# Moving work between the regimes of a graph-attention kernel: weight sums, aggregation steps and a softmax placed elsewhere

## The chip, the cores and the metric

The kernel runs on one core of one Trainium2 chip. The core has engines that work side by side, each through its own list of instructions in order: TensorE (PE in the profile, with its weight loads as PEld) multiplies matrices into the PSUM banks, VectorE (DVE) and ScalarE (ACT) work on elements, GpSimd (POOL) too, and SyncE (SP) issues the transfers. An engine waits where the next instruction of its list needs what another has not yet delivered. The metric is the device time of one launch in microseconds, the median of several runs. Before the change it is 1914.68 us (three runs from 1913.48 to 1915.18).

## What is computed

There are 64 graphs of 256 nodes with 512 features. Two layers follow each other, each with a residual and a layer norm over the features:

```python
# layer 0: neighbours averaged by degree, both halves multiplied by W
deg = jnp.sum(adj, axis=-1, keepdims=True)
agg = jnp.einsum('bij,bjf->bif', adj, x) / jnp.maximum(deg, EPS)
out = jnp.einsum('bnf,of->bno', jnp.concatenate([x, agg], axis=2), W)
x = _layernorm(x + jax.nn.relu(out), axis=-1)

# layer 1: a score for each node, a softmax over the 256 nodes of a graph
q, k = jnp.split(x @ Wqk, 2, axis=-1)
v = x @ Wv
agg = jnp.einsum('bij,bjd->bid', adj, k * mask[:, :, None])
w = inv_scale * mask * jnp.einsum('bid,bid->bi', q, agg)
x = _layernorm(x + jax.nn.softmax(w, axis=1)[:, :, None] * v, axis=-1)
```

## The kernel before

The graphs are taken in 32 pairs, and each turn of the loop, called a period here, does layer 0 of pair j and layer 1 of pair j - 1 in alternation. In layer 1 the product of the two halves of Wqk is formed once, so that a score is a row of x times that product times the aggregated x.

Every product is done by Strassen's method in Winograd's form: seven half-size products in place of eight, from sums of blocks of both factors. The sums of the weights W0 (layer 0) and W1 (layer 1) are made once at the start; those of x, of the adjacency and of the intermediate results in every period. The first two products and the fifth of an outer Strassen step are themselves split once more ("inner").

VectorE, ScalarE and GpSimd instructions keep the order in which the program writes them. Work that may lie anywhere, such as norms, degrees or sums, is put into named chains; a clock of the program, advanced by every product and used at build time only, decides after which product the next step of a chain is written:

```python
class InOrder:
    # ... (free: the modelled time at which this engine is done)
            self.free = max(self.free, self.clock[0]) + self.cost(name, size)
            return self.tc.keep_in_program_order(getattr(self.engine, name)(out, *args, **kwargs))
# ...
    def tick():                      # after a product: write steps that fit
        while not quiet[0]:
            for c in list(chains):   # chains in order of rank
                if c[2][0] <= clock[0] and c[3][0][0].free <= clock[0] + room[c[3][0][0]]:
                    step(c)
                    break
            else:
                return

    def flush(*names):               # write the rest of these chains now
        # ...
```

The sums of a weight are sixteen subtractions, four of them 1024 elements wide and twelve 256 wide:

```python
    def weight_sums(w, name):
        # ... b11, b21, b12, b22: quarters of w; t1, t2, t4, it: new tiles
        def inner_of(n, p, b):
            # ... c11 ... c22: quarters of b
            return [sub(i1, c12, c11), sub(i2, c22, i1), sub(c12, c22, c12), sub(i4, c21, i2)]
        work = ([sub(t1, b12, b11)] + inner_of(0, "P1", b11) + [sub(t2, b22, t1)] + inner_of(2, "P5", t1)
                + [sub(b12, b22, b12), sub(t4, b21, t2)] + inner_of(1, "P2", b21))
```

The profile leaves numbers out of names, so the tiles of both weights read as w, t and t_i.

Aggregation with the adjacency is called gather. Its seven steps have the letters a to g; tv are sums of the right factor, sa those of the adjacency:

```python
        def g5():                                    # c
            twice(p5, "S1", "T1")
        def u2():                                    # d
            twice(u, "S2", "T2", start=False)
            act.copy(r12, of(u))
        def u3():                                    # e
            twice(u, "S3", "T3", start=False)
            act.copy(r22, of(u))
            vec.tensor_add(r22, of(p5), r22)
        def g3():                                    # f
            twice(p5, "S4", "B22", start=False)
            vec.tensor_add(r12, of(p5), r12)
```

The step f adds on to the bank p5 that step e's addition has read before. The degrees of a pair need the adjacency by rows, which lies in the tile turn; ScalarE sums each row:

```python
        def degree(k, t):
            act.activation(r[:, k, t], r[:, k, t], AF.Copy, accum_out=deg[:, k, t:t + 1])
        def invert():
            vec.tensor_scalar(rdeg, deg, DEG_EPS, None, op0=OP.max)
            vec.reciprocal(rdeg, rdeg)
```

The norm of layer 0 is a chain of VectorE and ScalarE steps for each half of the graph: scale by the degree, residual (both scalar_tensor_tensor), statistics (bn_stats, bn_aggr), factor (ScalarE), shift (VectorE), scale (ScalarE), and the turning of the result (transpose into the tile turn, then 16 small transfers into x1T, which layer 1 multiplies).

The softmax of a pair takes the maximum, two exponentials for each graph, a reciprocal and a product, and then queues the additions of v to x ("adds") and the last norm ("finish"):

```python
        queue(0, "softmax", (vec, lambda: vec.reduce_max(top, rk, axis=AX.XY, negate=True)),
              (act, lambda: exp(0)), (act, lambda: exp(1)), (vec, divide))    # divide ends with finish(j)
```

For the last pair the softmax is done in another way: the scores are turned by TensorE (transpose), and the probabilities come out of a small product with the reciprocal of the total:

```python
        def divide(to):
            vec.reciprocal(total, total)
            for t in range(NT):
                tc.keep_in_program_order(nc.tensor.matmul(to[:, t:t + 1], e[:, t * P:(t + 1) * P], total, ...))
```

In the loop, run("i k ...") writes the products named by letters in that order; m, p, q, r, s belong to layer 0, and j, k, h, n, q, p and f to layer 1:

Of the kernel before, what the change touches and what calls it, by code (L numbers as in the profile page):

```python
# [94 lines left out]
def resnorm_kernel(  # L95
# [34 lines left out]
    clock, chains, shared, quiet = [0.0], [], [1.0], [False]  # L130
# [28 lines left out]
    def flush(*names):  # L159
        while True:  # L160
            c = next((c for c in chains if not names or c[1] in names), None)
            if not c:
                return
            step(c)

    def run(order, **units):
        for name in order.split():
            units[name].pop(0)()
# [87 lines left out]
    def weight_sums(w, name):  # L256


        b11, b21, b12, b22 = (w[:, k * H:(k + 1) * H, :] for k in range(4))
        t1, t2, t4 = (const.tile([P, H, F], F32, name=f"{name}{k}") for k in (1, 2, 4))  # L260
        it = const.tile([P, 3, 3, HF], F32, name=f"{name}i")
        sides = {"B22": b22, "T2": t2, "T3": b12, "T4": t4}
        sub = lambda *args: lambda: vec.tensor_sub(*args)

        def inner_of(n, p, b):
            c11, c12, c21, c22 = (b[:, e, h * HF:(h + 1) * HF] for e in range(2) for h in range(2))
            i1, i2, i4 = (it[:, r, n] for r in range(3))
            sides[p] = {"B11": c11, "B21": c21, "B22": c22, "T3": c12, "T1": i1, "T2": i2, "T4": i4}
# [3 lines that stand above are left out]
        return sides, work  # L272
# [35 lines left out]
    def mask_adj(j):  # L308
        def mask(k, t):
            act.activation(adjs[j][:, k, t], adjs[j][:, k, t], AF.Copy,  # L310
                           scale=mask_sb[:, 2 * j + k, t:t + 1])
        queue(4, "mask", *[(act, lambda k=k, t=t: mask(k, t)) for k in range(2) for t in range(NT)])

    def degrees(j):
        deg = small.tile([P, 2, NT], F32, name="deg")
        rdeg = rdegs[j] = small.tile([P, 2, NT], F32, name="rdeg")
        r = rows.pop(j)
# [7 lines that stand above are left out]
        queue(2, "degrees", *[(act, lambda k=k, t=t: degree(k, t)) for k in range(2) for t in range(NT)],  # L325
              (vec, invert))
# [335 lines left out]
    inner_sums(Xs[0], gp, 1)  # L662
    sumsA[0] = adj_sums(0)
    degrees(0)
    W1, work = weight_sums(w1, "t1_")
    queue(9, "w1", *[(vec, do) for do in work])
    pu, py, pf, pw = banks
# [2 lines left out]
    for j in range(NP):  # L670
        X = Xs.pop(j)
        flush("finish")
        owns[j] = pool.tile([P, 2, NT, F], F32, name="own", bufs=3)
        if j > 0:
            load_adj(j)
            run_now(late_sums)
            late_sums.clear()
            sumsA[j] = adj_sums(j)

        u, y, o = pf, py, pu  # L680
        ys[j] = pool.tile([P, 2, NT, F], F32, name="y")
        a1, a2, a3, a4, a5, a6, a7 = layer0(j, o, u, y)
        i = inner("P1", X, W0, pw[0], u, a1)
        k = inner("P5", X, W0, pw[1], y, a5)
        m = inner("P2", X, W0, pw[0], o, a2)
        p, q = pairs(u, X, S2, W0["T2"], a6), pairs(u, X, S3, W0["T3"], a7)
        r, s = pairs(y, X, S4, W0["B22"], a3), pairs(u, X, A22, W0["T4"], a4)
        if j == 0:
            run("i k i k i k i k", i=i, k=k)
            flush("degrees")  # L690
            load_rows(1)
        elif j == 1:
            run("i k i k i k i k", i=i, k=k)
            run("m p p m p p m", m=m, p=p)
            flush("norm")
            places[0](range(16))
        else:
            run("i f k", i=i, k=k, f=open1)
            send_scores(j - 2)
            run("i f k", i=i, k=k, f=open1)  # L700
            flush("norm")
            fetch_scores(j - 2)
            places[0](range(16))
            run("i f k i f k", i=i, k=k, f=open1)
        if j > 0:
            flush("mask")
            sumsM[j - 1] = adj_sums(j - 1)
            load_x(j)
            if j + 1 < NP:
                load_rows(j + 1)  # L710
        if j > 1:
            softmax(j - 2)
            shared[0] = 1.0
        if j != 1:
            run("m p p m p p m", m=m, p=p)
        run("q q q q m", m=m, q=q)
        if j > 0:
            Y = x1Ts.pop(j - 1)
            inner_sums(Y, gp, 0)
            sums_Y = (*outer_sums(Y, vec), (vec, lambda: inner_sums(Y, gp, 1)))  # L720
        if j > 1:
            queue(1, "sums", *sums_Y)
        run("r r r r", r=r)
        T = sums_T(ys[j])

        if j != 1 and j < NP - 1:
            degrees(j + 1)
        zs[j] = pool.tile([P, 2, NT, F], F32, name="z")
        g = gather(sumsA.pop(j), T, zs[j], pw[1], y[1], y[0])

        def load_next():
            if j == NP - 1:
                return
            if j > 0:
                load_xT(j + 1)
                shared[0] = 1.25
            inner_sums(Xs[j + 1], gp, 0)
            rest = outer_sums(Xs[j + 1], gp)
            run_now(rest[:1])
            inner_sums(Xs[j + 1], gp, 1)  # L740
            late_sums.extend(rest[1:])
        if j == 0:
            load_next()
            run("s s a b s c d e s g f", s=s, **g)
        else:
            u2, o2, y2 = o, pf, y
            b1, b2, b3, b4, b5, b6, b7, b8 = layer1(j - 1, ys[j][:, :, 0], o2, u2, y2)
            jj = inner("P1", Y, W1, pw[0], u2)
            k = inner("P2", Y, W1, y[0], o2, b2)
            if j == 1:  # L750
                run("s s a b s c d e s g f", s=s, **g)
                flush("w1")
                degrees(2)
                queue(1, "sums", *sums_Y)
                run("j k j k j k j", j=jj, k=k)
                b1(None)
                run("k", k=k)
            else:
                run("s s j a b s j c d s j e k j", s=s, j=jj, k=k, **g)
                quiet[0] = True  # L760
                run("k", k=k)
                quiet[0] = False
                b1(None)
                run("g f", **g)
        flush("softmax", "adds", "sums", "degrees")
        if j > 0:
            aggs[j - 1] = late.tile([P, 2 * N_SIDE], F32, name="agg").rearrange(
                "p (k t f) -> p k t f", k=2, t=NT)
            vs[j - 1] = [late.tile([P, NT, F], F32, name="v", bufs=2) for _ in range(2)]
            T = sums_T(owns[j - 1])  # L770
            g = gather(sumsM.pop(j - 1), T, aggs[j - 1], pw[0], o2[1], o2[0])
            h, q = pairs(u2, Y, S2, W1["T2"], b6), pairs(u2, Y, S3, W1["T3"], b7)
            n = inner("P5", Y, W1, pw[1], y2, b5)
            p, open1 = pairs(u2, Y, A22, W1["T4"], b4), pairs(y2, Y, S4, W1["B22"], b3)
            norm0(j)
            mask_adj(j)
            run("k h h" if j > 1 else "h h", k=k, h=h)
            load_next()
            run("n k" if j > 1 else "n", k=k, n=n)
            run("h h a n b q d q n c q e q p n g p f p", h=h, n=n, q=q, p=p, **g)  # L780
            b8()
            run("p", p=p)
            py, pu = pu, py
        else:
            norm0(0)
            mask_adj(0)


    j = NP - 1
# [27 lines left out]
    run("c d i m e i m g i f i", i=i, m=m, **g)  # L817
    v = pool.tile([P, 2, NT, F], F32, name="z")
    vs[j] = [v[:, k] for k in range(2)]
    run("m n h h", m=m, n=n, h=h)  # L820
    softmax(j - 1)
    run("m n h h n q q q q n", h=h, m=m, q=q, n=n)
    flush("softmax", "adds")
    run("p p p p", p=p)
    w = small.tile([P, 2, NT], F32, name="w", bufs=1)
# [4 lines left out]
        turn()  # L830
        exps()
    run("r r", r=r)
    flush()
    probs[j] = small.tile([P, 2, NT], F32, name="probs", bufs=2)
    for k in range(2):
        last[k][0](pw[k])
        vec.tensor_copy(probs[j][:, k], pw[k][:, :NT])
        b3(k)
    norms = []

    def close(k, t, scale):
# [40 lines left out]
```

## Time and profile before

| what | number |
|---|---|
| device time, median | 1914.68 us |
| span of the profiled execution | 1913.8 us |
| PE busy | 1881.3 us (98%) |
| PEld busy | 1248.8 us (65%) |
| DVE busy | 1587.1 us (83%) |
| ACT busy | 1061.6 us (55%) |
| POOL busy | 748.8 us (39%) |
| mean granted TensorE clock | 0.994 |
| moved by the transfers | 182.17 MB, 95 GB/s |

A share of busy time is an average over the whole span. The table says that TensorE is the busiest engine, but not where it waits. For that one takes three views: the waits, which give for each engine, tile and line what it waited for, how long in total and how often; the table by stretch, with the busy time of every engine in parts of the span; and the timeline, which lists the instructions of one engine in order, with the idle time before each and what ended it. Nearly all instructions have the same two lines, 90 (the recording helper) and 173 (the products), so they are told apart by their tiles: y and own are results of layer 0, z and agg those of the two gathers, v the values of layer 1, tv and sa the gather's sums.

### The profile page before, as it was taken

To read this page: it belongs to the slowest core of one execution; us is meant where nothing else is said; L and a number is where in the kernel's file an instruction comes from. 1 tells how busy PE (TensorE), PEld (TensorE's weight loads), DVE (VectorE), ACT (ScalarE), POOL (GpSimd) and SP (SyncE) were. 2 spreads that over 40 slices of the span, in tenths; PEclk is the share of its full clock that TensorE was granted. 3 is DMA by queue.
4 is the path that set the end of the run, shared out by engine and by line. 5 is a ranking of instruction groups with operands and counts; after the bars stand their busy time and mean duration, and the time that the engine had idled before them with its cause. 6 is when DMAs were issued, how large, how long until landed. Compare 5 with 4: busy or idle time off the path is not lost.

```text
span 1913.8 us, 22655 instructions
## 1 busy us (share of the span) xinstructions
PE 1881.3 (98%) x6596; PEld 1248.8 (65%) x6596; DVE 1587.1 (83%) x2952; ACT 1061.6 (55%) x2571; POOL 748.8 (39%) x898
## 2 busy tenths in 40 slices
PE   9899999999999999999999999999999999999996
PEld 4566666666666666666676666666666666666663
DVE  6879878889888888888889888888888898888885
ACT  3455555565555565655565655555655655555654
POOL 4344324444334444234444244443244343244420
PEclk9999999999999999999999999999999999999998
DMA  6223343433433423434433434433434333434311
GB/s 221 63 56 97 105 102 76 116 82 94 105 96 89 116 76 97 105 84 104 113 76 99 105 75 114 101 84 103 105 72 116 87 95 107 98 80 116 80 52 46
DMA packets 389147, 182.17 MB, mean 95 GB/s; under 512 B 272160, under 2 KB 353696, under 8 KB 389024
## 3 DMA queue, kind: packets, MB, share of 16 engines
q1 hardware_dynamic: 389024, 180.72, 36.4%
q8 instruction: 54, 0.88, 0.2%
q14 instruction: 69, 0.57, 0.1%
HBM read 114.10 MB, written 34.06 MB: 77 GB/s over the span
## 4 chain that ended last, share of the span: by engine, by line
PE 86%; DVE 5%; DMA 3%; POOL 2%; SPq 2%; issue 1%; ACT 1%; ACTq 0%; DVEq 0%; POOLq 0%
PE bank L173 86%; SPq L178 2%; DMA turn<-adj 1%; DVE own L90 1%; DMA xT<-x_t 1%; POOL xT_i L90 1%; POOL sa L90 1%; POOL xT_s L90 1%; DVE st L90 1%; DVE y L90 0%; ACT own L90 0%; DVE bank L90 0%; DMA x1T<-turn 0%; DVE tv L90 0%; DVE t_i L90 0%
## 5 line engine op out<-in xcount | busy, mean ns | idle before, releaser
L90 ACT COPY bank<-bank 128x256 f32<-128x256 f32 (+1 forms) x576 | 251.9, 437 | 248.5 <-PE bank L173 232.5
L90 POOL TENSOR_TENSOR xT_i<-xT 128x256 f32<-128x256 f32 x62 | 61.4, 990 | 530.7 <-DMA xT<-x_t 443.4
L173 PE MATMUL bank<-w,x1T_s 128*128 128x512 f32 x512 | 260.3, 592 | 0.0
L173 PE MATMUL bank<-w,xT_s 128*128 128x512 f32 x512 | 230.2, 592 | 1.3 <-DVE y L90 1.3
L90 ACT ACTIVATE own<-own,shift,rstd 128x512 f32<-128x512 f32 x256 | 197.8, 808 | 12.3 <-DVE shift L90 12.1
L90 POOL TENSOR_TENSOR x1T_i<-x1T 128x256 f32<-128x256 f32 x64 | 49.7, 776 | 393.2 <-DMA x1T<-turn 379.3
L173 PE MATMUL bank<-tv,sa 128*128 128x256 f32 x768 | 191.9, 379 | 1.4 <-issue 1.4
L90 DVE TENSOR_TENSOR y<-bank,y 128x512 f32<-128x512 f32 x192 | 128.6, 684 | 61.5 <-ACT y L90 57.2
L173 PEld LDWEIGHTS bank<-tv,sa 128*128 128x128 f32 x768 | 145.8, 190 | 49.2 <-issue 18.7
L90 ACT COPY y<-bank 128x512 f32<-128x512 f32 x192 | 109.1, 587 | 119.4 <-PE bank L173 116.7
L90 DVE BATCH_NORM_STATS2 st<-own 128x6 f32<-128x512 f32 x256 | 173.1, 676 | 2.4
L173 PEld LDWEIGHTS bank<-w,xT_s 128*128 128x128 f32 x512 | 97.2, 190 | 96.7 <-issue 86.0
L173 PE MATMUL bank<-t,xT_s 128*128 128x512 f32 (+1 forms) x384 | 158.8, 522 | 0.5 <-ACT own L90 0.5
L173 PE MATMUL bank<-t,x1T_s 128*128 128x512 f32 (+1 forms) x384 | 158.1, 521 | 0.3 <-ACT y L90 0.3
L90 ACT ACTIVATE turn<-turn 128x256 f32<-128x256 f32 x128 | 52.5, 411 | 174.0 <-DMA turn<-adj 174.0
L90 DVE TENSOR_TENSOR bank<-bank,fifth 128x256 f32<-128x256 f32 x256 | 97.3, 426 | 49.4 <-PE bank L173 45.2
L90 ACT COPY agg<-bank 128x512 f32<-128x512 f32 x128 | 74.6, 583 | 96.7 <-PE bank L173 95.9
L173 PE MATMUL bank<-t,x1T 128*128 128x512 f32 x256 | 125.2, 592 | 0.0
L90 POOL TENSOR_TENSOR sa<-adj 128x256 f32<-128x256 f32 x128 | 108.7, 849 | 36.0 <-ACT adj L90 27.4
L173 PE MATMUL bank<-t,xT 128*128 128x512 f32 x248 | 121.6, 592 | 0.0
L173 PE MATMUL bank<-t_i,x1T_i 128*128 128x256 f32 x384 | 114.8, 381 | 2.5 <-ACT bank L90 2.3
L173 PE MATMUL bank<-t_i,xT_i 128*128 128x256 f32 x384 | 115.4, 382 | 0.2
(144 smaller groups left out, 4172.3 us busy)
## 6 DMA issues: line engine op xcount, KB each, us to landing
x<-x SPq DMA_DIRECT2D x64, 512.0 KB, 4.9
xT<-x_t SPq DMA_DIRECT2D x62, 512.0 KB, 6.2
x1T<-turn SPq DMA_DIRECT2D x496, 64.0 KB, 2.3
out<-own SPq DMA_DIRECT2D x62, 512.0 KB, 4.8
adj<-adj_t SPq DMA_DIRECT2D x64, 256.0 KB, 3.0
turn<-adj SPq DMA_DIRECT2D x64, 256.0 KB, 5.1
row<-d SPq DMA_DIRECT2D x31, 256.0 KB, 4.7
wqk<-wqk_t SPq DMA_DIRECT2D x4, 512.0 KB, 5.5
```

Of the source, the lines that this page charges most:

```text
L90: return self.tc.keep_in_program_order(getattr(self.engine, name)(out, *args, **kwargs))
L173: tc.keep_in_program_order(nc.tensor.matmul(ps, a, b, start=start, stop=True, skip_group_check=True))
L178: return tc.keep_in_program_order(nc.sync.dma_start(out, in_))
```

## The change

The change moves instructions; none is added or taken away. It has four parts.

- **Sums of W1.** Before their chain is queued, the modelled time of VectorE (vec.free) is set to six microseconds after the clock. Up to there it had run far ahead, since every sum recorded in the setup counts. So the chain's steps are written sooner, beside the first products of period 0. What is left of the chain is held back during the end of that period and put back after it.
- **Aggregation steps.** In periods 0 and 1 the order of the steps changes from "a b s c d e s" to "a b c d s e s": a product s now stands between d and e.
- **Degrees of pair 2.** They are queued in period 1 after the norm, and not ahead of the first products of layer 1.
- **Softmax of the pair next to last.** It is queued four products sooner, and the remaining chains are written out after the last pair's probabilities and no longer ahead of them.

```diff
+    vec.free = clock[0] + 6.0
     W1, work = weight_sums(w1, "t1_")
     queue(9, "w1", *[(vec, do) for do in work])
@@ period 0
             load_next()
-            run("s s a b s c d e s g f", s=s, **g)
+            held = [c for c in chains if c[1] == "w1"]
+            chains[:] = [c for c in chains if c[1] != "w1"]
+            run("s s a b c d s e s g f", s=s, **g)
@@ period 1
-                run("s s a b s c d e s g f", s=s, **g)
+                run("s s a b c d s e s g f", s=s, **g)
                 flush("w1")
-                degrees(2)
                 queue(1, "sums", *sums_Y)
@@ periods from 1 on, layer 1
             run("k h h" if j > 1 else "h h", k=k, h=h)
+            if j == 1:
+                degrees(2)
+                flush("degrees")
             load_next()
@@ end of period 0
             norm0(0)
             mask_adj(0)
+            chains.extend(held)
@@ last pair
-    run("m n h h", m=m, n=n, h=h)
     softmax(j - 1)
-    run("m n h h n q q q q n", h=h, m=m, q=q, n=n)
+    run("m n h h m n h h n q q q q n", h=h, m=m, q=q, n=n)
     flush("softmax", "adds")
@@
     run("r r", r=r)
-    flush()
     probs[j] = small.tile([P, 2, NT], F32, name="probs", bufs=2)
     for k in range(2):
         last[k][0](pw[k])
         vec.tensor_copy(probs[j][:, k], pw[k][:, :NT])
         b3(k)
+    flush()
```

## The prediction

> **What bounds the kernel now.** I started with the list of waits, taken for TensorE alone. Its columns are the waiting engine, tile and line, what it waited for, the total in us, how often, and the longest.
>
> ```profile
> PE bank L576 <- DVE total L90: 4.9, 2, 3.9
> PE bank L173 <- DVE z L90: 4.0, 1, 4.0
> PE bank L173 <- ACT bank L90: 2.9, 6, 1.7
> PE bank L173 <- DVE y L90: 1.6, 2, 1.3
> PE bank L566 <- DVE w L90: 1.5, 1, 1.5
> PE bank L173 <- issue: 1.4, 2, 0.7
> ```
>
> All of TensorE's waits together are under 20 us of 1913.8. The table by stretch says where they lie (after the stretch and its length: busy us of PE, PEld, DVE, ACT, POOL, then granted clock, DMA share, GB/s).
>
> ```profile
> 30.00:40.00 10.00, 10.00 (x29) 5.32 (x28) 4.15 (x10) 5.03 (x15) 0.84 (x2) 1.00 0.37 107
> 50.00:57.00 7.00, 2.96 (x11) 1.78 (x11) 6.93 (x10) 1.76 (x3) 5.62 (x6) 0.85 0.00 0
> 57.00:64.00 7.00, 6.89 (x20) 5.08 (x20) 6.79 (x10) 2.63 (x8) 0.00 (x0) 0.66 0.00 0
> 130.00:600.00 470.00, 469.76 (x1657) 313.64 (x1656) 393.69 (x735) 267.77 (x654) 187.01 (x224) 1.00 0.38 97
> 1890.00:1900.00 10.00, 4.10 (x14) 1.86 (x12) 6.66 (x22) 4.93 (x12) 0.00 (x0) 0.90 0.14 51
> ```
>
> The reader is to see three regimes. From 130 to about 1890 us TensorE never stops: nothing that this change does elsewhere can shorten that part, and nothing there can swallow a gain made ahead of it, because work that arrives earlier is simply multiplied earlier. Before 130 us and after 1890 us VectorE sets the pace. And at 30 to 40 us VectorE is idle for almost six of ten microseconds, just before the stretch where TensorE waits for it.
>
> The timeline shows the wait itself, first TensorE, then VectorE (start, length, engine, line, operation; in brackets the idle time before it and what ended it):
>
> ```profile
> 51.57 1.11 PE L173 MATMUL bank<-tv,adj 128*128 128x256 f32 x4
> 56.73 2.05 PE L173 MATMUL bank<-y,sa 128*128 128x256 f32 x4 [4.04 <-DVE z L90]
> 58.57 1.06 PE L173 MATMUL bank<-t_i,xT_i 128*128 128x256 f32 x2
> ```
>
> ```profile
> 37.07 0.69 DVE L90 TENSOR_TENSOR y<-bank,y 128x512 f32<-128x512 f32 x1 [5.00 <-ACT y L90]
> 48.97 2.31 DVE L90 TENSOR_TENSOR t<-w,t 128x1024 f32<-128x1024 f32 x1
> 57.63 1.21 DVE L90 TENSOR_TENSOR t<-w,t 128x1024 f32<-128x1024 f32 x1
> 1898.18 0.16 DVE L90 SCALAR_TENSOR_TENSOR shift<-mv,rstd 128x2 f32<-128x2 f32 x1 [2.01 <-ACT rstd L90]
> ```
>
> The last aggregation product of period 0 (bank<-y,sa, step f) needs the second addition into z. VectorE gives that at 56.58, because it has put sums of W1 between: t at 48.97 and four quarter sums at 52.59. The last line is the tail: the softmax of the last pair stands behind a shift of the pair before it.
>
> **What the Trainium skill says.** "TensorE: Matmul & The Clock Gate", Part 1, What's actually happening, says that the array runs at half clock after about 3.4 us idle and at full clock after as much steady work. The trace agrees: after the 4.04 us gap two matmul pieces start every 0.85 us (58.57, 59.42, 60.27) where they otherwise take 0.43 us, and the granted clock is 0.66 for 57 to 64 us. "SBUF — State Buffer", SBUF: two separate sides, says that VectorE and GpSimd lock each other out of a shared port pair when a VectorE instruction has two SBUF inputs. The trace agrees: the same 128x1024 sum took 2.31 us beside a busy GpSimd and 1.21 us beside an idle one (both shown above). "Perfetto Trace Analysis", Optimization Strategy, advises interleaving regimes whose contended engines differ; that is what this change does with VectorE's idle 5.00 us.
>
> **The change part by part.**
>
> *1. Sums of W1 forward.* The order of the built program shows what resetting VectorE's modelled time does: eight quarter sums and the 1024-wide t_2 move into the idle time before y at 37.07. GpSimd is idle there, so 8 x 0.34 us (their pitch, 73.00 to 73.33) + 1.15 = 3.9 us, from 32.0 to about 36. It fits; no delay. The other two 1024-wide sums (1.21 us free, up to 2.3 beside GpSimd) go to 38 and 42 us in place of four quarter sums which took 0.8 + 1.8 us there: nothing gained or lost by 44.9, when the sums tv begin. After tv (end 49.04) VectorE goes straight to z, rdeg, z: 0.6 + 0.9 + 0.7 us, so z is ready at about 51.3 rather than 56.58.
>
> *2. The s steps spread (period 0).* d and e share one bank, and e waits 0.72 us (the "issue" wait) while ScalarE empties it. An s product now stands between. TensorE then reaches f at about 51.5. So f starts at 51.5 rather than 56.73: 5.2 us, and with no idle gap the clock stays full. From 56.73 to 67.59 TensorE did 40 pieces, worth 40 x 0.215 = 8.6 us, in 10.9; that is 2.3 us more. On TensorE's side 7.5 us.
>
> *3. What VectorE gives back.* VectorE is full from 49 to 78, so its own saving decides. Removed there: 2.23 + 3.31 + 2.31 = 7.85 us of issue time (48.97, 52.59, 56.50). But the norm of pair 0 now starts at 53 rather than 59.5, while GpSimd runs until 55.7. Two or three instructions with SBUF inputs then take about 1.7 instead of 0.7 us (the like pair at 107.64 and 109.42 took 1.75 and 1.65), which takes 2 us back. So the four "bank<-bank,fifth" come at 60.7 rather than 66.13; TensorE, there at about 61, waits about 1 us for them, a new wait. The shift is 5.4 us, and it lasts through the y wait at 78.03 (1.26 us, kept).
>
> *4. Period 1.* The spread s steps remove the 0.72 us at 88.45. The degrees of pair 2 move back: in the trace ScalarE waits for their rows (turn<-adj, landing at 95.2), and the copies queued behind them hold TensorE 1.68 us at 96.06. Both go: 5.4 + 0.72 + 1.68 = 7.8 us. The four degree activations (0.41 us each) now precede a bank copy later on, 1.65 us of delay against 2.6 us of other products (h h a): no wait. The wait for agg at 119.28 (1.25 us) stays and may grow by 0.5, since GpSimd's sums follow a load that moves less than TensorE. **Start: 7.3 us.**
>
> *5. Softmax of the pair next to last.* The maximum moves to where VectorE idles 3.54 us (before 1878.45), the four exponentials to ScalarE's gaps. VectorE does four additions (2.74) and three statistics (2.46) from 1882.0 to 1887.4, where it idled 3.28 us. Then fifth adds 0.77, z 1.28, dot 0.73, a statistic 0.85, dot 0.75, w 0.16: w ends at about 1891.9 rather than 1892.27. Transposes at 1891.95, the last two r products until 1894.1; beside them maximum and exponentials end by 1893.6. So the product with the reciprocal (L576) starts at about 1894.15 rather than 1898.55, and the 15.3 us behind it stay. **Tail: 4.4 us.**
>
> Sum: 7.3 + 4.4 = 11.7 us; 1914.7 - 11.7 = 1903.0.
>
> **The rivals.** *TensorE's view:* all removed waits count whole, with the clock loss: 7.5 + 0.7 + 1.7 + 4.4 = 14.3, so 1900.4. For it: GpSimd may finish sooner when VectorE leaves it alone. Against: VectorE's 6.79 busy of 7 at 57 to 64. *VectorE stays the bound of the start:* moved sums collide with GpSimd's sums at 39 to 49 and delay tv, the new wait at 61 grows to 2 or 3 us, and turn and x1T come late; start 4, so about 1906.5. For it: tv's last sum took 1.75 us beside GpSimd. Against: as much work moves out of 42 to 44 as into it. *The tail turns into another wait:* the moved additions delay z<-bank and thereby r, or the two 512 KB stores now leave 2 us nearer the end relative to the final stores; tail 2, so 1905.4. For it: z would be done at 1888.8, just when r starts; against: the stores landed in 4.8 us, and 15 us remain. *A steady-state wait swallows it:* speaks against it that TensorE waits 0.8 us in all from 130 to 1850.
>
> **Range and chances.** The centre is 1903.0. With start between 4.5 and 9.5 and tail between 3 and 5 I get 1900 to 1907; I take 1899.5 to 1907. Two per cent are 38 us, more than all of TensorE's waits, so a change over 2% is all but excluded either way.
>
> **What would show each step right or wrong.** Step 1: VectorE's 5.00 us before y at 37.07 filled, tv still starting near 45. Step 2: f near 51.5, both 0.72 us waits gone, granted clock 1.00 from 50 to 64. Step 3: a TensorE wait of about 1 us for own near 61; without it the first rival is right. Step 4: no 1.68 us wait for ScalarE. Steady part: the same length from the first product of period 2 to the end of the last p. Step 5: 15.3 us from the first L576 to the end, and less than 4 us from the transposes to it rather than 6.2. Wrong would be the whole if tv started over 1 us later, or if the lead shrank between 130 and 1890 us.

## The result, and the profile after

The changed kernel takes 1900.05 us (median; 1899.3 to 1900.65) beside 1914.5 us for the kernel before, measured together: a ratio of 0.9925 with a 95% interval of 0.9912 to 0.9937, or 14.45 us less. Measured a second time the ratio was 0.9928 (0.9915 to 0.9942). The time lies inside the predicted range of 1899.5 to 1907, near its lower end; the gain is 2.75 us larger than the forecast of 11.7.

The span in the profile fell from 1913.8 to 1898.0 us. The waits of TensorE alone, the costliest of them, show what is left (engine, tile and line, what it waited for: total us, times, longest):

```profile
PE bank L173 <- ACT own L90: 2.9, 2, 1.6
PE bank L173 <- DVE agg L90: 1.3, 1, 1.3
...
PE bank L173 <- DVE y L90: 1.0, 1, 1.0
PE bank L576 <- DVE total L90: 0.9, 1, 0.9
PE bank L566 <- DVE w L90: 0.8, 1, 0.8
```

The 4.0 us for z and both "issue" waits are gone, and the waits for the reciprocals of the last pair fell from 4.9 to 0.9. Of the two waits for own, the one of 1.30 us at 60.90 us is new. The other, 1.57 us at 29.76 us, lies ahead of all that the change moves; before it was 0.46 us at the same place, and TensorE came there later because its first products took 16.76 us in that execution and 15.61 in this one. The table by stretch, with the same columns as before:

```profile
30.00:40.00 10.00, 10.00 (x29) 5.37 (x29) 8.41 (x17) 5.09 (x15) 0.79 (x2) 1.00 0.36 107
50.00:57.00 7.00, 6.89 (x30) 5.40 (x30) 5.33 (x8) 5.05 (x13) 5.68 (x6) 1.00 0.00 1
57.00:64.00 7.00, 5.70 (x22) 3.58 (x21) 6.83 (x15) 3.73 (x11) 1.78 (x2) 1.00 0.00 0
```

VectorE's busy time from 30 to 40 us has doubled, 4.15 to 8.41: that is the moved sums. TensorE is busy 6.89 of 7 us where it was 2.96, and its granted clock is 1.00 in both later stretches (before 0.85 and 0.66). The timeline, TensorE first:

```profile
51.12 1.03 PE L173 MATMUL bank<-y,sa 128*128 128x256 f32 x4
60.90 1.95 PE L173 MATMUL bank<-t,xT_s 128*128 128x512 f32 x4 [1.30 <-ACT own L90]
1883.56 0.60 PE L576 MATMUL bank<-total,fifth 1*128 1x1 f32 x4
1885.07 0.60 PE L576 MATMUL bank<-total,fifth 1*128 1x1 f32 x4 [0.91 <-DVE total L90]
```

```profile
37.12 0.69 DVE L90 TENSOR_TENSOR y<-bank,y 128x512 f32<-128x512 f32 x1 [0.93 <-ACT y L90]
52.91 1.13 DVE L90 SCALAR_TENSOR_TENSOR own<-z,rdeg,own 128x512 f32<-128x512 f32 x1
54.08 1.10 DVE L90 SCALAR_TENSOR_TENSOR own<-own,x 128x512 f32<-128x512 f32 x1
```

Step f starts at 51.12 instead of 56.73, VectorE's idle time before y shrank from 5.00 to 0.93 us, and y itself starts where it did.

To compare profiles I cut the span at the first product of step f in layer 1's gather (bank<-own,sa) of period 1 and at the same product of period 31. "Start" is its time in period 1, "steady" the time from there to period 31, "tail" the rest.

| kernel | ratio to before (95%) | start | steady | tail |
|---|---|---|---|---|
| before | 1 | 119.3 | 1736.4 | 58.1 |
| changed, first profile | 0.9925 (0.9912 to 0.9937) | 110.4 | 1735.0 | 52.6 |
| changed again | 0.9928 (0.9915 to 0.9942) | 111.7 | 1736.0 | 52.6 |
| e1: sums alone | 0.9973 (0.9965 to 0.9982) | 114.4 | 1737.6 | 57.7 |
| e2: changed, old step order | 0.9936 (0.9924 to 0.9949) | 111.7 | 1736.8 | 52.6 |
| e3: changed, degrees back | 0.9951 (0.9939 to 0.9964) | 114.2 | 1736.0 | 52.6 |
| e4: tail alone | 0.9975 (0.9965 to 0.9984) | 119.7 | 1736.4 | 52.6 |
| e5: softmax sooner alone | 0.9966 (0.9952 to 0.9980) | 120.8 | 1736.2 | 52.6 |
| e6: chains later alone | 0.9996 (0.9988 to 1.0005) | 121.1 | 1737.9 | 57.2 |
| e7: gap filled | 0.9989 (0.9982 to 0.9995) | 119.3 | 1735.2 | 58.1 |
| e8: rest of the sums held | 0.9923 (0.9909 to 0.9936) | 111.3 | 1736.3 | 52.6 |
| e9: fifth sums sooner | 0.9931 (0.9919 to 0.9944) | 110.9 | 1737.3 | 52.6 |
| e10: both | 0.9921 (0.9908 to 0.9935) | 111.0 | 1736.3 | 52.6 |
| e12: degrees alone | 0.9988 (0.9981 to 0.9994) | 117.3 | 1735.3 | 58.1 |

The kernels before, e4, e5 and e6 are the same up to the end of the start, and it ended between 119.3 and 121.1 us. So a single start is good to about 1 us either way; the ratios and the single waits decide. A part of this scatter can be placed: nine of the fourteen profiles have a delay of 0.7 to 1.8 us in the transfers of period 1, and before, the changed kernel's first profile, e2, e3 and e9 don't have it (last section). Starts are best compared within these two groups.

### The profile page after: what moved, and what is told of

Read it like the earlier page. It is cut to its first block, busy times and chain, and to the rows that moved or that the text cites. A ratio compares the mean times of both kernels' runs of the same rounds, so it can differ in the third digit from the quotient of the medians.

```text
span 1898.0 us, 22655 instructions
## 1 busy us (share of the span) xinstructions
PE 1875.2 (99%) x6596; PEld 1246.5 (66%) x6596; DVE 1588.2 (84%) x2952; ACT 1061.1 (56%) x2571; POOL 752.3 (40%) x898
## 4 chain that ended last, share of the span: by engine, by line
PE 91%; DVE 4%; DMA 1%; SPq 1%; POOL 1%; issue 1%; ACT 0%; ACTq 0%; DVEq 0%; POOLq 0%
PE bank L173 91%; DVE own L90 1%; SPq L178 1%; DMA w<-w_t 1%; DVE st L90 1%; DVE y L90 0%; DVE tv L90 0%; DMA xT<-x_t 0%; DVE t_i L90 0%; DVE bank L90 0%; POOL xT_i L90 0%; POOL sa L90 0%; ACT own L90 0%; DMA turn<-adj 0%; POOL xT_s L90 0%
## 5 line engine op out<-in xcount | busy, mean ns | idle before, releaser
L90 ACT ACTIVATE turn<-turn 128x256 f32<-128x256 f32 x128 | 52.6, 411 | 169.2 <-DMA turn<-adj 169.2
L173 PE MATMUL bank<-t_i,x1T_i 128*128 128x256 f32 x384 | 114.4, 380 | 0.7 <-POOL x1T_i L90 0.4
```

The source lines that it names most:

```text
L173: tc.keep_in_program_order(nc.tensor.matmul(ps, a, b, start=start, stop=True, skip_group_check=True))
```

## The experiments

**e1, sums of W1 alone.** The kernel before with the first part:

```diff
+    vec.free = clock[0] + 6.0
     W1, work = weight_sums(w1, "t1_")
@@ period 0
+            held = [c for c in chains if c[1] == "w1"]
+            chains[:] = [c for c in chains if c[1] != "w1"]
             run("s s a b s c d e s g f", s=s, **g)
@@ end of period 0
+            chains.extend(held)
```

> The kernel before with the first part alone: sums of W1 forward, the rest of their chain held back during the end of period 0; step order, degrees and tail as before. My theory (VectorE sets the pace from 50 to 78 us): step f starts near 51.8 instead of 56.73, the granted clock stays 1.00 there, a new wait for own of about 0.6 us comes near 60, the two 0.72 us waits stay, TensorE's lead is 6 us at the y wait and stays there, because the wait for the degrees of pair 2 (1.68 us) stays or grows: 1908.5 in all. Rival (TensorE's own waits decide): a lead of 7.5 us, 1907. Rival (the sums moved collide with GpSimd's and return as a later wait): a lead under 3 us, 1911.5 or more.

f started at 52.13, the clock stayed up, TensorE waited 1.10 us for own and 0.99 us for y, and its lead over before at the y wait was 6.1 us (71.96 against 78.03). At the end of the start it was 4.9 us against the profile of before, and 5.3 to 6.7 against e4, e5 and e6, which have the delayed transfers, as e1 has. The wait for the bank behind the degrees is 2.20 us here and 1.68 in before, but 2.02 to 2.27 in e4 to e6, where the start is that of before: nothing says that it grew with this part. The time fell by 0.27%, 5.2 us (3.4 to 6.7). Both rivals fall, the one with 7.5 us and the one with less than 3.

**e2, the old order of the steps** in both periods of the changed kernel ("a b s c d e s").

> The changed kernel with the old step order a b s c d e s in both periods. My theory: e comes 0.7 us later, so VectorE's second addition to z, f and the norm come 0.7 us later too, and the same again in period 1: 1901.5, 1.4 us more than the changed kernel. Rival: in period 0 TensorE waits 1.30 us for own anyway, and that wait only shrinks to 0.6, so that 0.7 us are lost in all: 1900.8.

Both 0.72 us waits came back. f started at 52.00 in period 0 (0.88 later) and at 84.99 in period 1 (1.54 later than in the changed kernel), so the own wait, now 1.08 us, did not absorb it. The start is 1.3 us longer than in the changed kernel's first profile, near the expected 1.4; the second profile has the same 111.7, but with the delayed transfers, which e2 does not have. The ratio rose by 0.0011, about 2 us, and the two intervals overlap. The waits are settled; how much of them reaches the end isn't, by the times.

**e3, degrees of pair 2 back** ahead of the first products of layer 1, all else changed.

> The changed kernel with the degrees of pair 2 queued where they were, ahead of the first products of layer 1. My theory: the rows land as late after the turning as before, while TensorE comes to these products 0.85 us sooner relative to it, so the wait for a bank that ScalarE copies returns as 1.68 + 0.85 = 2.5 us and is kept to the end: 1902.4. Rival: VectorE is full from 92 to 120 us, so the wait for agg (1.33 us) shrinks by as much, and only 1 us is lost: 1901.0.

This was a miss on the large side: 0.9951, a loss of 5.0 us against the changed kernel's 0.9925, twice what I expected; with both intervals it is about 2 to 8 us. ScalarE's timeline of this run, then TensorE's:

```profile
88.96 0.42 ACT L90 ACTIVATE turn<-turn 128x256 f32<-128x256 f32 x1 [3.25 <-DMA turn<-adj]
```

```profile
89.79 0.70 PE L173 MATMUL bank<-t_i,x1T_i 128*128 128x256 f32 x2 [3.18 <-ACT bank L90]
```

The table by stretch of the same run:

```profile
90.00:93.00 3.00, 2.90 (x9) 2.11 (x9) 0.00 (x0) 2.14 (x9) 0.46 (x1) 0.71 0.22 68
```

ScalarE stands 3.25 us before rows that have not landed, TensorE waits 3.18 us for the bank copies queued behind, and then the granted clock is 0.71: the 6.53 us from 89.79 to the end of the next wait take 4.84 in the kernel before (96.06 to 100.90). So 3.2 + 1.7 us are lost at this place. TensorE's waits for agg then shrank from 0.48 and 1.33 us to 0.86 in all, as the rival had it, and at the end of the start 3.9 us are left (114.2 against 110.4). The rows were issued at 82.9 and took 6 us. TensorE's wait begins 7.8 us sooner than before (86.61 against 94.38), while the rows landed only 6.3 us sooner (88.96 against 95.23): so the same order costs 1.5 us more of waiting than it cost before.

**e12, degrees of pair 2 alone,** in the kernel before:

> The kernel before with the degrees of pair 2 moved and nothing else. The wait of 1.68 us behind them goes and no wait takes its place: 1.7 us less, 1912.8. Undoing this part in the changed kernel cost 4.7 us in the medians (3.18 us of wait and slow products after it), so if the parts simply added, 4 us or more would show here; I expect that they don't add: the wait is longer in the changed kernel because TensorE arrives sooner there, relative to the rows.

The wait went, and behind it only an agg wait of 0.51 us is new, which e5 and e7 also have with the degrees where they were: 0.9988, or 2.3 us (1.1 to 3.6), near the expected 1.7. Undoing the part cost 5.0 us in e3. The longer wait there (3.18 us) speaks for a part that is worth more once the first is in, but the intervals overlap, so the times don't show it. The sums, the degrees and the tail alone gave 5.2 (e1), 2.3 (e12) and 4.8 us (e4, next), and the step order is worth about 2 (e2): that is some 14.4, as much as the whole change, so a plain sum of the parts is not ruled out.

**e4, e5 and e6, the tail.** e4 is the kernel before with both tail edits:

```diff
-    run("m n h h", m=m, n=n, h=h)
     softmax(j - 1)
-    run("m n h h n q q q q n", h=h, m=m, q=q, n=n)
+    run("m n h h m n h h n q q q q n", h=h, m=m, q=q, n=n)
...
-    flush()          # ahead of the last probabilities
+    flush()          # after them
```

> The kernel before with the last part alone: softmax of the pair next to last sooner and the remaining chains written after the last probabilities. My theory (the regimes are independent): start and steady part as before, from the first turning product of the last pair to the end 5.5 us less than before, 1909.0. Rival (the tail gained through the earlier start, or the early runs differ by chance in the steady part): 1910.5 or more, or a tail shorter by less than 4.5 us.

The tail shrank from 58.1 to 52.6 us, 5.5 us less, as in the changed kernel; start and steady part are those of before. The time fell to 0.9975, by 4.8 us (3.1 to 6.7). The tail does not need the earlier start. e5 has the softmax sooner and the flush where it was:

> The kernel before with the softmax of the pair next to last queued sooner, but the remaining chains still written out ahead of the last probabilities. With both tail edits the scores w end 0.8 us after the r products and the first product with the reciprocal (L576) starts 2.25 us after the transposes. If the order of VectorE decides (my theory), this edit alone brings nearly all: the shifts of the earlier pair come before the reciprocal but their factors are long there, while the four scalings of ScalarE now stand ahead of nothing it needs. Expected 5 us less than before, 1909.5; the two kernels' tails equal within 0.5 us. If it is the late writing of the chains that counts, 2 us or less.

The same 52.6 us: with the softmax sooner, the later flush adds nothing that shows. e6 has only the flush moved:

> The kernel before with only the remaining chains written after the last probabilities; softmax where it was. Expected by my theory: the wait for the shift (2.01 us, for ScalarE's factor behind two scalings) leaves the path to the reciprocal, but the four statistics stay in front of it, so the first product with the reciprocal starts at most 2.3 us sooner; the second one gains 0.4 us more where the clock stays full; 2 to 2.5 us less than before, 1912.5. If the two edits are each the whole gain, 5 us less.

It gained 1.0 us of the expected 2 to 2.5 in the tail, and nothing that the ratio can tell from zero. Its timeline, TensorE's first, then VectorE's:

```profile
1899.57 0.60 PE L576 MATMUL bank<-total,fifth 1*128 1x1 f32 x4 [1.57 <-DVE total L90]
```

```profile
1904.55 0.16 DVE L90 SCALAR_TENSOR_TENSOR shift<-mv,rstd 128x2 f32<-128x2 f32 x1 [2.01 <-ACT rstd L90]
```

The first reciprocal product did start 2.3 us sooner relative to the product of period 31 (40.5 us after it, before 42.9). But the shift with its wait of 2.01 us now stands ahead of the last additions, and takes most of it back. The earlier softmax is what takes this wait out, since ScalarE's factors are then done in time.

**e7, the gap filled.** The kernel before, with four unread products in front of f in period 0:

```diff
-            run("s s a b s c d e s g f", s=s, **g)
+            run("s s a b s c d e s g", s=s, **g)
+            for _ in range(4):
+                tc.keep_in_program_order(nc.tensor.matmul(pw[0], X.chunk(A22, 0, 0), W0["T4"][:, 0], start=True,
+                                                          stop=True, skip_group_check=True))
+            run("f", **g)
```

> The kernel before with four products that nobody reads (0.86 us each, into the bank that the next product overwrites) put into TensorE's wait of 4.04 us ahead of step f in period 0. They add 3.4 us of work inside the gap, and leave the time of z and so of f as it is. If the slow products after the gap are a matter of the clock, the granted clock stays 1.00 from 57 to 64 us and the stretch from f to the fifth sums takes 8.6 us instead of 10.9; VectorE, busy in 6.79 of 7 us there, then holds TensorE at the own copies for most of it, and about 1 us is left at period 1. If the slowness comes from something else (weight loads, VectorE), the stretch stays at 10.9 us.

The table by stretch of this run, and TensorE's timeline (line 746 is the added products):

```profile
57.00:64.00 7.00, 6.89 (x31) 5.50 (x32) 6.79 (x10) 4.26 (x11) 0.00 (x0) 1.00 0.00 1
```

```profile
52.67 3.60 PE L746 MATMUL bank<-t,xT 128*128 128x512 f32 x8
56.89 1.10 PE L173 MATMUL bank<-y,sa 128*128 128x256 f32 x4 [0.63 <-DVE z L90]
```

With TensorE kept at work the clock stays 1.00, and f and the products up to own take 8.4 us (56.89 to 65.28); before they took 10.9, and 9.8 to 11.0 in e4, e5, e6 and e12, which have the same gap. So the slow products come from the idle gap. f is no sooner, and TensorE then waits 0.68 us for own and 1.35 for y: the y wait ends at 76.74, in the five profiles with the gap at 76.99 to 78.30, so 0.3 to 1.6 us are left and VectorE takes back the rest. The time is 0.11% less (0.05 to 0.18%), 2.1 us, with more work for TensorE. One of the 20 executions took 7142.62 us, for no cause that the record shows, and is left out of the ratio.

**e8, the rest of the sums held.** In the changed kernel the chain of W1 is put back just ahead of its flush in period 1, so that the last four quarter sums leave the stretch at 65 us.

> The changed kernel with the last four quarter sums of W1 held until they are needed, in VectorE's idle time near 80 us, instead of 64.6 to 66.8 us. If VectorE alone sets the pace there, 2.1 us less work takes the y wait (0.99 us) away and all of it is gained: 1899.0. My theory: ScalarE's factor and scalings of the second graph (from 67.0 us on) end last once VectorE is faster, so only about 0.5 us of the wait goes: 1899.5. If neither bounds, no change of the wait.

TensorE's timeline of this run:

```profile
70.82 3.67 PE L173 MATMUL bank<-w,xT_s 128*128 128x512 f32 x8 [0.60 <-DVE y L90]
84.50 0.70 PE L173 MATMUL bank<-t_i,x1T_i 128*128 128x256 f32 x2 [0.34 <-POOL x1T_i L90]
```

The y wait fell from 0.99 to 0.60 and not to nothing: the second shift then waits 0.50 us for ScalarE's factor, as I had expected. Behind it TensorE waits 0.34 us for x1T_i; this profile has the delayed transfers. The time is not distinguishable from the changed kernel's.

**e9, the four fifth sums sooner,** by a modelled cost of 1.4 for VectorE from the end of period 0 until they are written.

> The changed kernel with the four additions bank<-bank,fifth written two norm instructions sooner in period 1, by raising VectorE's modelled cost to 1.4 from the end of period 0 until these products are written. The same work in another order. If VectorE as a whole sets the pace from 50 to 71 us (my theory), TensorE's wait for own (1.30 us) shrinks to about 0.2 and its wait for y grows by as much, from 0.99 to about 2; lead and time unchanged, 1900. If only the order counted, the wait would be gained: 1.1 us less, 1898.9.

TensorE's timeline of this run:

```profile
71.64 3.67 PE L173 MATMUL bank<-w,xT_s 128*128 128x512 f32 x8 [2.72 <-DVE y L90]
```

The own wait of 1.30 us vanished, and the y wait grew from 0.99 to 2.72. So the order of VectorE's instructions is not the limit from 53 to 71 us; another order only moves the wait. In the changed kernel VectorE is idle there once, for 0.88 us, while ScalarE scales ahead of the last turning, and e8 has shown that ScalarE's factor is only some 0.4 us behind. VectorE's work is the limit, with ScalarE close behind it. Nothing was gained; the ratio is 0.9931.

**e10, both,** with the last four quarter sums put into VectorE's idle time at 79 us:

> The same, and the last four quarter sums of W1 written between the second and third addition into z of period 1, where VectorE idles 3.4 us, so that neither the stretch from 64 to 67 us nor the one before the x1T sums carries them. By my theory the wait for own falls to 0.2, and the wait for y stays near 0.6, since ScalarE's factors come sooner with the products; the lead at step f of period 1's second gather is 9.5 to 10 us instead of 8.9; 1899.2. If the turning and the transfers into x1T end last, TensorE waits for x1T_i instead and nothing is gained: 1900.

TensorE came to the x1T products sooner, and waited there (TensorE's timeline of this run):

```profile
84.82 0.70 PE L173 MATMUL bank<-t_i,x1T_i 128*128 128x256 f32 x2 [1.13 <-POOL x1T_i L90]
```

TensorE passed this point at 84.82, 0.3 us later than in e8 (84.50). That looks like the rival, but this profile can't decide for it: its 16 transfers were issued 0.8 us sooner than the changed kernel's, and the first sum x1T_i came 14.4 us after the first of them, where the changed kernel's first profile took 12.55. With 12.55 us this sum, which took 0.72, would have ended at 82.9, and TensorE came at 83.7: an estimate from these profiles, by which it would not have waited. The ratio of 0.9921 is not distinguishable from the changed kernel's, so whether e10 gains anything stays open. No version beat the changed kernel clear of noise.

**The changed kernel again.**

> The changed kernel once more, for a second profile. In the first one TensorE's lead over the kernel before grew from 8.93 us at the last aggregation product of period 1 to 10.28 us at that of period 31, in 1735 us in which no instruction differs. If this is chance of a single execution (my theory: other kernels' profiles moved by -0.4 to +0.5 us there, in both directions), the lead at the end is 8.5 to 9.5 us this time and the start and the tail repeat within 0.2 us: 8.9 at period 1, and 52.6 us from the product of period 31 to the end. If the change has an effect there, the lead grows by 1 us or more again. The time ratio to before repeats as 0.9925.

The steady part took 1736.0 us, so 1.0 of the 1.4 us that the first profile gained there did not come back, and the scatter of the fourteen profiles (1.4 us below before and 1.5 above, more than I had put) covers the rest. I missed on the start: it was 111.7, not 110.4. Up to the y wait it repeats (71.13 against 71.14). Then x1T_i made TensorE wait 0.53 us, because this execution has the delayed transfers, and ScalarE's agg copy 1.12 us instead of 0.48.

## Why the prediction was right, and where its sizes were off

*What bounds.* Right in the main. The steady part neither gave nor took: 1735.0 to 1737.9 us in all profiles, the kernel before in the middle. e4 and e1 show that tail and start can be had apart. That VectorE sets the pace up to 130 us is too broad, as step 4 itself says: between 80 and 100 us TensorE waited for copies behind late rows (1.68 us in before) and, in the changed kernel's second profile, for small transfers (0.53 us).

*Step 1* held: the sums filled the idle time, y did not move, and tv started at 44.29 rather than near 45.

*Step 2* held: f at 51.12 (51.5 predicted), both waits gone, clock 1.00. Of the 5.6 us by which f came sooner, 0.9 are the step order's (e2). e7 shows that the lost clock belonged to the gap; at full clock the products from f to own took 8.4 us, 8.6 predicted.

*Step 3* held in mechanism, and one term was too large. The new wait for own came at 60.90 with 1.30 us (about 1 near 61 predicted), the y wait stayed, at 0.99 for 1.26, and e9 shows that VectorE's work and not its order is behind both. But I took 2 us back for the norm's first instructions beside GpSimd, at 1.7 us each. They took 1.13 and 1.10, so 0.8 us went back. The lead at the own wait was 6.7 us (67.59 to 60.90), not 5.4.

*Step 4* held: no wait behind the degrees. The lead at the products after them was 9.7 us (100.90 to 91.22), against 7.8 predicted: 6.9 at the y wait (78.03 to 71.14) where I had put 5.4, mostly the term of step 3, then the 0.72 and 1.68 as predicted, and 0.4 that is not broken down. Then the agg waits, 0.48 and 1.33, took 0.75 back, 0.5 predicted for the second of them. The start came out at 8.9 and 7.6 us less than the profile used for the prediction, against 7.3; that profile happens to have the shortest start of the four equal ones.

*Step 5* held, and was too small: 5.5 us instead of 4.4. The first reciprocal product started 4.7 us sooner than before relative to period 31 (4.4 predicted). The rest is the chain behind it, which I took to stay 15.3 us. It took 14.4, mostly because each of the two reciprocal groups took 0.60 us instead of 0.98: the granted clock is 0.50 from 1898.50 to 1901.50 us before, and 1.00 from 1883.50 to 1886.50 us after. In e12, where the 3.90 us wait stands before it, TensorE's timeline has the slow form again; e1, with the same wait, has it in the second group only:

```profile
1895.43 0.98 PE L576 MATMUL bank<-total,fifth 1*128 1x1 f32 x4 [3.90 <-DVE total L90]
```

```profile
1894.84 0.57 PE L576 MATMUL bank<-total,fifth 1*128 1x1 f32 x4 [3.90 <-DVE total L90]
1896.42 0.98 PE L576 MATMUL bank<-total,fifth 1*128 1x1 f32 x4 [1.00 <-DVE total L90]
```

With 1.57 us of wait ahead of the first group (e6), or none, both take 0.60. I had counted the clock at the first gap and left it out at the second.

Of the rivals, TensorE's view named the nearest number, 1900.4, for a reason that did not hold: the removed waits did not count whole, since the own wait came and e9 could only move it. That it came closest is luck: its start was 1.0 us too large (9.9 against 8.9) and its tail 1.1 too small (4.4 against 5.5). VectorE as the bound of the start (1906.5) had the right engine, but the moved sums did not collide with GpSimd's. The tail's new waits (own stores, z ahead of r) did not appear.

## What to carry to other kernels

Look for the stretches with different limits first, and fill an engine's idle time just ahead of the stretch where it is the limit; what is saved outside the stretch that TensorE fills reaches the end, until the next engine in that stretch takes over. A wait on TensorE costs more than its length where the clock falls behind it, so look for slow products after every gap, the last one included. And a wait can grow when the work ahead of it shrinks: the one behind the degrees was 1.68 us in the kernel before, and 3.18 with the rest of the change in, as TensorE came 7.8 us sooner and the rows only 6.3.

## What the runs showed of the hardware

The lost clock varies between executions of the same instructions. After the gap of 4.04 to 4.06 us ahead of f the granted clock from 57 to 64 us was 0.66 in the kernel before, 0.76 in e4 and 0.60 in e6; e6's y wait ended at 78.28 and e4's at 76.99. The Trainium skill, "TensorE: Matmul & The Clock Gate", Part 1, What's actually happening, says that the activity window runs freely, which fits this scatter, though no run here shows the window itself. It gives about 3.4 us of idle time as what halves the clock; here the clock also fell after shorter gaps, in some executions and not in others. After a wait of 2.25 us for the bank behind the degrees e6 ran at 0.65 from 98 to 101 us, and e5, after 2.27 us, at 1.00. The table by stretch of e6, then of e5:

```profile
98.00:101.00 3.00, 3.00 (x11) 2.45 (x10) 0.00 (x0) 1.73 (x5) 1.12 (x2) 0.65 0.30 96
```

```profile
98.00:101.00 3.00, 3.00 (x15) 2.65 (x14) 0.35 (x2) 2.41 (x8) 1.16 (x2) 1.00 0.33 101
```

Next to last in each line is the DMA share, ahead of it the clock; the code up to there is the same. What decides between them was not tried.

The transfers scatter too. GpSimd forms the sums x1T_i from what the 16 small transfers of the turned result bring. From the issue of the first transfer to the first of these sums, period 1 took 12.5 to 12.6 us in five profiles (before, the changed kernel's first, e2, e3, e9) and 13.3 to 14.4 us in the other nine. GpSimd's timeline shows this sum in the changed kernel's first and second profile and in e10, where the first transfers were issued at 70.45, 70.44 and 69.66 us:

```profile
83.00 0.73 POOL L90 TENSOR_TENSOR x1T_i<-x1T 128x256 f32<-128x256 f32 x1 [17.08 <-DMA x1T<-turn]
```

```profile
84.22 0.72 POOL L90 TENSOR_TENSOR x1T_i<-x1T 128x256 f32<-128x256 f32 x1 [18.32 <-DMA x1T<-turn]
```

```profile
84.04 0.72 POOL L90 TENSOR_TENSOR x1T_i<-x1T 128x256 f32<-128x256 f32 x1 [20.38 <-DMA x1T<-turn]
```

The DMA table, taken for just this stretch, differs in one row. The nine slower profiles all have one packet there on the queue that the profile calls instruction. In the changed kernel's second profile, from 70.44 to 84.22 us (packets, MB, share):

```profile
q8 instruction: 1, 0.02, 0.5%
```

Of the five others four have none there, and in e2 it starts only when the last packet of the 16 transfers has ended (83.19 against 83.17 us). No run moved this packet, so it goes with the delay in fourteen profiles of fourteen, but is not shown to cause it.
